# An LSTM layer on one core: one load of 128 rows a step in place of four of 32, and a tail of six Strassen pairs and two plain steps

## The chip, the cores and the metric

The kernel runs on one core of a Trainium2 chip. The metric is the device time of one execution in microseconds (us); of several executions the median is taken. Everything is 32-bit floating point. TensorE (PE) multiplies matrices, VectorE (DVE) and ScalarE (ACT) work on tiles of 128 partitions in the on-chip memory (SBUF) and in the eight accumulation banks of TensorE (PSUM), GpSimd (POOL) does a little elementwise work, and the queue of SyncE (SP) issues nearly all transfers (DMAs) between DRAM and SBUF. A transfer is cut into packets that 16 DMA engines carry.

## The reference

An LSTM over 512 steps with a batch of 32 and 512 inputs and 512 hidden units; the layer's input is added to its output.

```python
xW = jnp.einsum('ntd,dg->ntg', x, Wx) + b          # x is 32 x 512 x 512, Wx is 512 x 2048
def step(carry, xw_t):                             # 512 steps, one after the other
    prev_h, prev_c = carry
    a = xw_t + prev_h @ Wh                         # Wh is 512 x 2048
    i = jax.nn.sigmoid(a[:, :Hd])
    f = jax.nn.sigmoid(a[:, Hd:2 * Hd])
    o = jax.nn.sigmoid(a[:, 2 * Hd:3 * Hd])
    g = jnp.tanh(a[:, 3 * Hd:])
    next_c = f * prev_c + i * g
    next_h = o * jnp.tanh(next_c)
    return ((next_h, next_c), next_h)
return x + hs                                      # hs: all next_h
```

## The kernel before, in words

**The step.** The 512 hidden units are four blocks j of 128. A tile of a step has 128 partitions (j, b): block j, batch row b, 32 rows for each j; its 512 columns are the four gates of the block's units, so that all of a step is one PSUM bank of 128 x 512. `h_part(t)` multiplies the previous h by Wh: 16 instructions of 512 columns, each in one quarter (32 rows) of the array and four of them side by side, into the banks `gbank` (`gbank_72`, `gbank_73`); the trace has two records for each instruction of PE, so that it counts 32. Before that, `seed_step` has ACT copy the step's row of x.Wx + b from SBUF (`xw`) into the bank, so that the product lands on it. `cell` is then the chain of ACT (sigmoid, tanh) and DVE instructions that ends in the transposed h of the next step (`ht`). That chain takes part of the step, and PE fills the wait with work that nothing waits for at once: the products of x and Wx for steps that come later.

**x.Wx.** For the steps 18 to 497 it is made in 15 groups of 32 steps by a scheme of 26 products of sums of blocks, each of which is cut by Strassen's scheme into seven. Its left sums lie in `ubuf`, its right sums are read row by row from DRAM (`vdram`) into a ring of three rows (`vring`), its products go to five PSUM banks (`xbank_66` to `xbank_70`) and to `bbank`, and ACT and DVE add them up (`cbuf`, `r`). Finished blocks of the result are stored to DRAM in `xwd` (`xwd_85` and `xwd_86`, a group each in turn) as [8, 128 rows, 4 blocks j, 512 columns]: the 128 rows are 4 steps by 32 batch rows. `load_xw` reads a step back, at step t that of step t + 3, into one of the three slots of `xw`. This goes on at one pace from about step 20 to step 466; below it is called the stream. The first 18 steps (the head) and the last 14 (the tail, from step 498) have their x.Wx made by other code. From step 469 on (`SPLIT`) a step is done in two halves of 64 hidden units of each block, by 32 instructions of 256 columns, on two pairs of banks (`xbank_66`, `xbank_67` and `gbank_72`, `gbank_73`).

**The tail.** Class `Tail` makes the x.Wx of the last 14 steps between the split steps. Two steps are a pair: Strassen's scheme makes them with seven products instead of eight. A product is eight instructions of 256 columns and is listed as four units, which PE does one by one (eight instructions of 128 columns for two units) or by twos. Plain, a step takes four such products. In the tail `xs_79`, `r_74`, `cbuf`, `ubuf` and a part of `vring` hold the blocks of Wx and their differences, and another part of `vring` the sums of x that the pairs need. The blocks are loaded at the end of the stream: some by `late_loads` at the steps that `LATE` lists, the last six by two calls of `tail.load(3)`, three blocks a call and two DMAs a block. `tail.fill(n)` emits the next n units of the list ahead of the chain of a step, and stops at a unit whose seed or sums don't stand yet.

**The order of the work.** Up to step 20 the instructions are recorded by a planner (`Plan`) that lists each engine's by due times that it estimates. After that each engine's instructions stand in the order in which the program writes them, and each waits for its inputs and for its buffer. SP has one queue for all its DMAs, in program order: a DMA that must wait for its input holds up those behind it.

Of the kernel before, what the change touches and what calls it, by code (L numbers as in the profile page):

```python
# [15 lines left out]
B = 32  # L16
T = 512
NJ = 4
# [4 lines left out]
W = G * P  # L23
HW = G * H
# [15 lines left out]
STREAM0 = HEAD + GS - AHEAD  # L40
END = HEAD + GS * NG - AHEAD
SPLIT = END + 2
LATE = (452, 454, 456, 462, 464, 466, 466)

FIRST = (13, 14, 15)
EARLY = (5, 6, 7, 8, 9, 10, 11, 12, 0, 1, 2, 3, 4, 13, 14, 15)
# [79 lines left out]
class Plan:  # L126
# [57 lines left out]
    def add(self, engine, op, call, out, ins):  # L184
        if not self.live:
            call()
            return
        self.ops.append((engine, op, call, out, ins))
# [220 lines left out]
def kernel(  # L409
# [156 lines left out]
    HALVES = [slice(0, H), slice(H, P)]  # L566

    PAIRS = [[xbank[0], xbank[1]], [gbank[0], gbank[1]]]
    LAST = [xbank[2], xbank[3]]

    def is_split(t):
        return t >= SPLIT
# [481 lines left out]
    def load_xw(t):  # L1054
        dst = xw[:, t % 3]
        if t < HEAD:
            nc.sync.dma_start(out=dst, in_=kept[t - PARKED])
            return
        g, n = divmod(t - HEAD, GS)
        assert group(g).stored[n // 8] == 4, (t, group(g).stored)  # L1060
        m, q = divmod(n, 4)
        for j in range(NJ):
            nc.sync.dma_start(out=dst[j * B : (j + 1) * B], in_=xwd[g % 2][m, q * B : (q + 1) * B, j])

    xw_late = {}

# [112 lines left out]
    class HeadPair:  # L1179
# [28 lines left out]
        def begin(self, first):  # L1208
            step = cbuf[:, 8, 2]
            if first:  # L1210
                sub(step, bias_full[:, HW:W], bias_full[:, 0:HW])
            nc.scalar.copy(self.lo, bias_full[:, 0:HW])
            nc.scalar.copy(self.hi, step)
            a, b = (x_plain(t).rearrange("p (k i) b -> p k i b", i=2) for t in self.steps)
            s1, s2, s3, s4 = (self.sums[:, i] for i in range(4))
            add(s1, b[:, :, 0], b[:, :, 1])
            sub(s2, s1, a[:, :, 0])
            sub(s3, a[:, :, 0], b[:, :, 0])
            sub(s4, a[:, :, 1], s2)
# [56 lines left out]
    class Tail:  # L1276

        def __init__(self):
            self.at = T - TAIL
            self.long_ops = 0.0  # L1280
            self.sums = vring[:, 0, 3:5].rearrange("p n (s k b) -> p n s k b", s=4, k=2)
            self.seed = vring[:, 0, 1:3].rearrange("p k c -> p (k c)")
            self.units = []
            self.results = {}
            self.done = set()
            self.banks = [xbank[2], xbank[3], xbank[4]]
            last = TAIL // 2 - 1
            for kos in ((0,), (1,)):
                for n in (0, 1):
                    self.product(n, 1, kos)  # L1290
            self.after(lambda: self.open(0))
            for n, r in ((2, 1), (0, 2), (1, 2)):
                self.product(n, r)
            self.after(lambda: self.open(1))
            for n in range(last + 1):
                if n > 1:
                    self.product(n, 2)
                if n > 2:
                    self.product(n, 1)
                self.product(n, 5)  # L1300
                self.after(lambda n=n: self.corners(n))
                self.after(lambda n=n: self.top(n))
                if n:
                    self.product(n - 1, 7)
                    self.after(lambda n=n: self.low(n - 1))
                self.product(n, 3)
                if n == 0:
                    self.after(lambda: self.left_sums(1))
                if n < last:
                    self.product(n, 6)  # L1310
                    self.after(lambda n=n: self.right(n))
                if n:
                    self.product(n - 1, 4)
                    self.after(lambda n=n: self.finish(n - 1))
                    if n < last:
                        self.after(lambda n=n: self.begin(n + 1))
            self.product(last, 6)
            self.after(lambda: self.right(last))
            self.paired = len(self.units)
            self.product(last, 7)  # L1320
            self.after(lambda: self.low(last))
            self.product(last, 4)
            self.total = len(self.units)
            self.making = list(range(4))
            self.loading = [b for b in range(2 * NJ) if b in V_OF]

        def steps(self, n):
            return self.at + 2 * n, self.at + 1 + 2 * n

        def after(self, f):  # L1330
            self.units[-1][2].append(f)

        def sum_of(self, blk):
            n = SUMS_AT.index(blk)
# [31 lines left out]
            return self.sum_of(blk)[:, {5: 0, 6: 1, 7: 2, 4: 3}[r]]  # L1366

        def product(self, n, r, kos=(0, 1)):
            needs = {1: "begin" if n > 2 else None, 3: "corners", 6: "corners", 7: "right", 4: "low"}.get(r)
            needs = needs and (needs, n)  # L1370
            for ko in kos:
                for q in range(2):
                    self.units.append((lambda m, ko=ko, q=q: self.matmuls(n, r, ko, q, m), q, [], needs))

        def matmuls(self, n, r, ko, q, m):
            cols = slice(q * P, (q + m) * P)
            bank = self.banks[n % 3]
            dst = bank[:, 0:HW]
            if r == 2:
                dst = bbank[:, n % 2 * HW : (n % 2 + 1) * HW]  # L1380
            elif r in (5, 3):
                dst = bank[:, HW:W]
            for j in range(NJ):
                nc.tensor.matmul(
                    dst[j * B : (j + 1) * B, cols],
                    self.left(n, r, ko),
                    self.right_side(r, ko * 4 + j)[:, cols],
                    start=r == 2 and ko == 0 and q == 0,
                    stop=True,
                    skip_group_check=True,  # L1390
                )

        def start(self, banks):
            for bank in banks:
                nc.scalar.copy(bank[:, 0:HW], bias_full[:, 0:HW])

        def open(self, n):
            if n == 0:
                nc.scalar.copy(self.seed[:, 0:HW], bias_full[:, 0:HW])
                sub(self.seed[:, HW:W], bias_full[:, HW:W], bias_full[:, 0:HW])  # L1400
                self.left_sums(0)
            for bank in self.banks[n : 2 * n + 1]:
                nc.scalar.copy(bank[:, HW:W], self.seed[:, HW:W])

        def begin(self, n):
            self.done.add(("begin", n))
            if n > 2:
                nc.scalar.copy(self.banks[n % 3], self.seed)
            self.left_sums(n)

        def left_sums(self, n):
            self.long_ops = 2000.0 if 0 < n < 3 else 0.0
# [7 lines left out]
        def corners(self, n):  # L1420
            self.done.add(("corners", n))
            self.results[n] = buf_of(take(free_c))
            nc.scalar.copy(self.results[n][:, 0:4:3], self.banks[n % 3].rearrange("p (n c) -> p n c", n=2))

        def top(self, n):
            self.long_ops = 2000.0 if n == 0 else 0.0
# [2 lines left out]

        def right(self, n):  # L1430
            self.done.add(("right", n))
            t, bank = self.results[n], self.banks[n % 3]
            nc.scalar.copy(t[:, 1], bank[:, 0:HW])
            add(t[:, 1], bank[:, HW:W], t[:, 1])
            self.keep(n, 0)

        def low(self, n):
            self.done.add(("low", n))
            t = self.results[n]
            add(t[:, 3], self.banks[n % 3][:, 0:HW], t[:, 3])  # L1440
            if self.steps(n)[1] == T - 1:
                nc.scalar.copy(half_of(T - 1, 1), t[:, 3])

        def finish(self, n):
            t = self.results[n]
            nc.scalar.copy(t[:, 2], self.banks[n % 3][:, 0:HW])
            self.keep(n, 1)

        def keep(self, n, i):
            xw_late[self.steps(n)[i]] = self.results[n][:, 2 * i : 2 * i + 2].rearrange("p s c -> p (s c)")  # L1450

        def share(self, t):
            gone = self.total - len(self.units)
            if gone < self.paired:
                return -(-(self.paired - gone) // max(1, T - 3 - t))
            return -(-(self.total - gone) // max(1, T - 1 - t))

        def fill(self, due):
# [15 lines left out]
    with tc.manual_schedule():  # L1474
# [75 lines left out]
        for t in range(T):  # L1550
# [129 lines left out]
                w_op()  # L1680
            if t == SPLIT - 9:
                late_weights[0] = True
            for _ in range(LATE.count(t)):
                late_loads.pop(0)()
            emit_matmuls(n)
            load_v_ahead()
            if t == SPLIT - 1:
                load_xw(t + 4)
            if END - 1 <= t <= END:
                tail.load(3)  # L1690
            if END <= t < SPLIT:
                tail.start(tail.banks[:2] if t == END else tail.banks[2:])
            done = tail.fill(0 if t < END else max(0, 10 - n // 2) if t < SPLIT else tail.share(t))
            cell(t)
            for f in done:
                f()
# [63 lines left out]
```

## Time and profile before

| | |
|---|---|
| median of 3 executions | 3055.44 us (3054.16 to 3058.35) |
| the profiled execution, its own time | 3056.29 us |
| its span, from the first to the last instruction | 3054.1 us |
| PE busy | 3045.8 us of the span |
| DVE, ACT busy | 2371.6 and 1482.6 us |
| DMA | 754.45 MB in 321,716 packets |
| loads of x.Wx (`xw<-xwd`) | 1920, of 64.0 KB each |
| time from issue to landing of one of them, median | 4.4 us |

How it is to be read. One execution was recorded by the hardware profiler. PE's busy time counts a matmul from its start to its modelled end, and successive ones overlap, so that PE reads as busy nearly everywhere; an idle stretch of PE shows in its own timeline with the engine that it waited for in brackets. All instructions are issued through one helper, so that every one has the line number L146, and groups are told apart by their tiles: `xw<-xwd` is a DMA that writes the tile `xw` and reads `xwd`. The digits of the line DMA are the mean busy share of the 16 DMA engines in tenths, in 40 equal slices of the span; they do not show one engine apart from another.

### The profile page before, as it was taken

The numbers are of one execution on the slowest core, as the hardware profiler recorded it, in microseconds if no ns is written. First come the engines' busy times: TensorE is split into PE (matmuls) and PEld (weight loads), VectorE is DVE, ScalarE is ACT, GpSimd is POOL, SyncE is SP. The second block draws the span as 40 slices with busy tenths as digits, with TensorE's granted clock in tenths as the row PEclk, the third lists the DMA queues.
The fourth block names the chain that finished last, engine by engine and source line by source line (L and its number), as shares of the span: only waits on it lengthen the run. The fifth ranks groups of instructions, "written<-read, shape, count | busy, mean of one in ns | idle before, by whom it ended". The sixth has DMA issues, their size and how long they took to land.

```text
span 3054.1 us, 107775 instructions
## 1 busy us (share of the span) xinstructions
PE 3045.8 (100%) x43344; PEld 1624.6 (53%) x43344; DVE 2371.6 (78%) x6556; ACT 1482.6 (49%) x5527; POOL 222.4 (7%) x473
## 2 busy tenths in 40 slices
PE   9999999999999999999999999999999999999999
PEld 6445555555555555555555555555555555555666
DVE  8778787887878878787787877878778787787765
ACT  2445444454454544545445454454544445454454
POOL 0000000000000000000000000000000000000000
PEclk9999999999999999999999999999999999999999
DMA  9988887787877878778787777777777777778630
GB/s 356 312 282 284 257 271 242 249 260 239 266 242 244 272 229 272 238 246 266 236 269 239 247 261 243 257 249 251 257 242 259 242 255 255 247 255 276 199 97 18
DMA packets 321716, 754.45 MB, mean 247 GB/s; under 512 B 51136, under 2 KB 106432, under 8 KB 320704
## 3 DMA queue, kind: packets, MB, share of 16 engines
q1 hardware_dynamic: 321072, 747.54, 74.8%
q8 instruction: 342, 5.60, 0.8%
q14 instruction: 158, 1.29, 0.2%
q10 hardware_dynamic: 144, 0.01, 0.0%
HBM read 565.94 MB, written 184.55 MB: 246 GB/s over the span
## 4 chain that ended last, share of the span: by engine, by line
PE 97%; DMA 1%; DVE 1%; SPq 0%; ACT 0%; issue 0%; ACTq 0%; DVEq 0%
PE gbank L146 54%; PE xbank L146 37%; PE bbank L146 6%; DMA xwd<-cbuf 0%; DMA ubuf<-vdram 0%; SPq L146 0%; DMA vring<-vdram 0%; DMA xnat<-in_x_dram 0%; DVE cbuf L146 0%; DVE prod L146 0%; DVE ubuf L146 0%; DMA xw<-xwd 0%; DVE s L146 0%; ACT s L146 0%; DVE hbuf L146 0%
## 5 line engine op out<-in xcount | busy, mean ns | idle before, releaser
L146 PE MATMUL gbank<-wh_sb,ht 128*32 128x512 f32 x14912 | 1697.6, 592 | 0.5
L146 PEld LDWEIGHTS gbank<-wh_sb,ht 128*32 128x32 f32 x14912 | 552.6, 110 | 807.3 <-issue 699.9
L146 ACT ACTIVATE s<-gbank 128x128 f32<-128x128 f32 (+1 forms) x1920 | 331.6, 257 | 1191.4 <-PE gbank L146 1189.9
L146 PE MATMUL xbank<-vring,ubuf 128*32 128x256 f32 (+1 forms) x13584 | 849.1, 368 | 0.0
L146 PEld LDWEIGHTS xbank<-vring,ubuf 128*32 128x32 f32 x13584 | 521.1, 110 | 297.2 <-issue 134.9
L146 DVE TENSOR_TENSOR prod<-s 128x128 f32<-128x128 f32 (+2 forms) x1093 | 296.9, 278 | 461.5 <-ACT s L146 457.1
L146 POOL TENSOR_TENSOR oc<-xnat,ht 128x128 f32<-128x128 f32 x469 | 222.2, 474 | 2637.4 <-DVE ht L146 1328.5
L146 ACT ACTIVATE tanh_c<-s 128x64 f32<-128x64 f32 (+1 forms) x921 | 236.9, 258 | 187.5 <-DVE s L146 184.3
L146 ACT COPY cbuf<-xbank 128x256 f32<-128x256 f32 (+1 forms) x692 | 287.8, 439 | 33.2 <-PE xbank L146 26.2
L146 ACT COPY gbank<-xw 128x512 f32<-128x512 f32 (+1 forms) x487 | 285.6, 589 | 1.6 <-DMA xw<-xwd 1.1
L146 DVE STREAM_TRANSPOSE ht<-hbuf 128x64 f32<-128x64 f32 (+1 forms) x921 | 226.8, 246 | 64.4 <-DVE hbuf L146 1.8
L146 DVE TENSOR_TENSOR s<-prod 128x64 f32<-128x64 f32 (+1 forms) x1007 | 227.4, 226 | 34.2
L146 DVE TENSOR_TENSOR cbuf<-xbank,cbuf 128x256 f32<-128x256 f32 x461 | 181.3, 409 | 41.6 <-ACT cbuf L146 39.5
L146 DVE TENSOR_TENSOR cbuf<-cbuf 128x1024 f32<-128x1024 f32 x171 | 208.8, 1224 | 0.7
L146 PE MATMUL xbank<-vring,r 128*32 128x256 f32 (+1 forms) x3216 | 208.3, 357 | 0.0
L146 PE MATMUL xbank<-vring,xs 128*32 128x256 f32 (+1 forms) x3120 | 201.9, 356 | 0.0
L146 DVE TENSOR_TENSOR hbuf<-o,tanh_c 128x64 f32<-128x64 f32 (+1 forms) x921 | 190.5, 207 | 4.6 <-ACT tanh_c L146 4.0
L146 ACT COPY r<-xbank 128x256 f32<-128x256 f32 (+1 forms) x425 | 180.8, 438 | 16.0 <-PE xbank L146 14.1
L146 PE MATMUL bbank<-vring,ubuf 128*32 128x256 f32 (+1 forms) x2600 | 184.4, 342 | 0.0
L146 PEld LDWEIGHTS xbank<-vring,r 128*32 128x32 f32 x3216 | 122.6, 110 | 79.6 <-issue 46.2
L146 ACT ACTIVATE o<-gbank 128x128 f32<-128x128 f32 (+1 forms) x508 | 154.7, 305 | 12.7 <-PE gbank L146 12.7
L146 PEld LDWEIGHTS xbank<-vring,xs 128*32 128x32 f32 x3120 | 118.9, 110 | 59.7 <-issue 22.9
(194 smaller groups left out, 2290.1 us busy)
## 6 DMA issues: line engine op xcount, KB each, us to landing
vring<-vdram SPq DMA_DIRECT2D x310, 896.0 KB, 5.8
xw<-xwd SPq DMA_DIRECT2D x1920, 64.0 KB, 4.4
xwd<-cbuf SPq DMA_DIRECT2D x139, 512.0 KB, 4.4
xwd<-r SPq DMA_DIRECT2D x86, 512.0 KB, 4.4
out_dram<-oc SPq DMA_DIRECT2D x255, 128.0 KB, 3.8
xnat<-in_x_dram SPq DMA_DIRECT2D x63, 512.0 KB, 5.3
xs<-in_x_grouped_dram SPq DMA_DIRECT2D x45, 512.0 KB, 4.8
vring<-vdram SPq DMA_DIRECT2D x33, 512.0 KB, 4.8
```

What stands on the lines that cost most here:

```text
L146: self.plan.add(self.name, op, lambda: call(*args, **kw), out, rest)
```

## The change

Two things are changed.

`load_xw` loads a step with one DMA. Before, a loop over j issued four, each of 32 rows of 2 KB: batch rows 0 to 31 of block j, to 32 neighbouring partitions. Now the block of DRAM is read as [j, b, columns], and one DMA of 256 KB writes all 128 partitions. In DRAM a row of the step (j, b) still lies 2 KB from the next j and 8 KB from the next b. As the instruction carries them, the pattern of the source has 4 blocks (2 KB apart) of 32 rows (8 KB apart) of 512 columns, and that of the destination 128 partitions of 512 columns. Before, both patterns had 32 rows of 512 columns.

The tail's 14 steps become a plain step (498), six pairs (499 to 510) and another plain step (511), where they were seven pairs: 4 + 42 + 4 = 50 products where there were 49. The plain products of step 498 and a quarter of those of 511 go to the bank `xbank_68`; the pairs have two banks in turn (`xbank_69` and `xbank_70`) where they had three. The plain products need no sums of x. The results of two pairs' steps are told of at once (`finish`), step 511 is seeded with what is finished of it and the rest of its products are added to its own banks (`plain_last`, `seed_last`). `tail.load(3)` is called at steps 467 and 468 instead of 466 and 467, one load of weights in `LATE` moves from step 466 to 467, and the number of units ahead of the chains of 467 and 468 may be up to 13 instead of 10 (`SPLIT` and `END` stay at 469 and 467).

```diff
@@ constants @@
-LATE = (452, 454, 456, 462, 464, 466, 466)
+LATE = (452, 454, 456, 462, 464, 466, 467)
...
-    LAST = [xbank[2], xbank[3]]
+    LAST = [xbank[3], xbank[4]]
@@ load_xw @@
         m, q = divmod(n, 4)
-        for j in range(NJ):
-            nc.sync.dma_start(out=dst[j * B : (j + 1) * B], in_=xwd[g % 2][m, q * B : (q + 1) * B, j])
+        nc.sync.dma_start(out=dst, in_=xwd[g % 2][m, q * B : (q + 1) * B].rearrange("b j c -> j b c"))
@@ class Tail @@
             self.units = []
+            self.late = []
             self.results = {}
             self.done = set()
-            self.banks = [xbank[2], xbank[3], xbank[4]]
+            self.banks = [xbank[3], xbank[4]]
             last = TAIL // 2 - 1
-            for kos in ((0,), (1,)):
-                for n in (0, 1):
-                    self.product(n, 1, kos)
-            self.after(lambda: self.open(0))
-            for n, r in ((2, 1), (0, 2), (1, 2)):
-                self.product(n, r)
-            self.after(lambda: self.open(1))
-            for n in range(last + 1):
+            self.plain(self.at, (0,))
+            self.after(lambda: self.begin(0))
+            self.plain(self.at, (1, 2, 3))
+            self.product(0, 1)
+            self.product(0, 2)
+            self.after(lambda: self.begin(1))
+            self.product(1, 2)
+            self.product(1, 1)
+            for n in range(last):
                 if n > 1:
                     self.product(n, 2)
-                if n > 2:
                     self.product(n, 1)
                 self.product(n, 5)
                 self.after(lambda n=n: self.corners(n))
                 self.after(lambda n=n: self.top(n))
-                if n:
+                if n == 0:
+                    self.plain(T - 1, (0,))
+                else:
                     self.product(n - 1, 7)
                     self.after(lambda n=n: self.low(n - 1))
                 self.product(n, 3)
                 if n == 0:
                     self.after(lambda: self.left_sums(1))
-                if n < last:
-                    self.product(n, 6)
-                    self.after(lambda n=n: self.right(n))
+                self.product(n, 6)
+                self.after(lambda n=n: self.right(n))
                 if n:
                     self.product(n - 1, 4)
                     self.after(lambda n=n: self.finish(n - 1))
-                    if n < last:
+                    if n + 1 < last:
                         self.after(lambda n=n: self.begin(n + 1))
-            self.product(last, 6)
-            self.after(lambda: self.right(last))
+            self.product(last - 1, 7)
+            self.after(lambda: self.low(last - 1))
+            self.product(last - 1, 4)
+            self.after(lambda: self.finish(last - 1))
+            self.after(self.seed_last)
             self.paired = len(self.units)
-            self.product(last, 7)
-            self.after(lambda: self.low(last))
-            self.product(last, 4)
+            self.plain_last((1, 2, 3))
             self.total = len(self.units)
             self.making = list(range(4))
             self.loading = [b for b in range(2 * NJ) if b in V_OF]
 
         def steps(self, n):
-            return self.at + 2 * n, self.at + 1 + 2 * n
+            return self.at + 1 + 2 * n, self.at + 2 + 2 * n
 
         def after(self, f):
             self.units[-1][2].append(f)
+
+        def plain(self, t, chunks):
+            bank = xbank[2]
+            needs = ("plain", self.at) if t > self.at else None
+            for c in chunks:
+                for q in range(4):
+                    self.units.append((lambda m, c=c, q=q: plain_part(t, c, q, m, bank, True), q % 2, [], needs))
+            if chunks[-1] == 3 or t == T - 1:
+                self.after(lambda: self.whole(t, bank))
+
+        def plain_last(self, chunks):
+            for c in chunks:
+                for q in range(4):
+                    half = q // 2
+                    emit = lambda m, c=c, q=q, half=half: plain_part(T - 1, c, q, m, LAST[half], place=q % 2)
+                    self.units.append((emit, q % 2, [], ("seeded", T - 1)))
+
+        def seed_last(self):
+            self.done.add(("seeded", T - 1))
+            for i in range(2):
+                nc.scalar.copy(half_of(T - 1, i), xw_late[T - 1][:, i * HW : (i + 1) * HW])
+
+        def whole(self, t, bank):
+            self.done.add(("plain", t))
+            nc.scalar.copy(self.room(t), bank)
+            if t == self.at:
+                nc.scalar.copy(bank, bias_full)
+
+        def room(self, t):
+            if not self.late:
+                buf = buf_of(take(free_c))
+                self.late += [buf[:, 0:2], buf[:, 2:4]]
+            xw_late[t] = self.late.pop(0).rearrange("p s c -> p (s c)")
+            return xw_late[t]
 
         def sum_of(self, blk):
             n = SUMS_AT.index(blk)
...
-        def start(self, banks):
-            for bank in banks:
-                nc.scalar.copy(bank[:, 0:HW], bias_full[:, 0:HW])
-
-        def open(self, n):
+        def begin(self, n):
+            self.done.add(("begin", n))
             if n == 0:
                 nc.scalar.copy(self.seed[:, 0:HW], bias_full[:, 0:HW])
                 sub(self.seed[:, HW:W], bias_full[:, HW:W], bias_full[:, 0:HW])
-                self.left_sums(0)
-            for bank in self.banks[n : 2 * n + 1]:
-                nc.scalar.copy(bank[:, HW:W], self.seed[:, HW:W])
...
+            nc.scalar.copy(self.banks[n % 2], self.seed)
+            if n != 1:
+                self.left_sums(n)
...
-                return -(-(self.paired - gone) // max(1, T - 3 - t))
+                return -(-(self.paired - gone) // max(1, T - 4 - t))
@@ the loop over the steps @@
-            for _ in range(LATE.count(t)):
+            if t in LATE:
                 late_loads.pop(0)()
             emit_matmuls(n)
             load_v_ahead()
             if t == SPLIT - 1:
                 load_xw(t + 4)
-            if END - 1 <= t <= END:
+            if END <= t < SPLIT:
+                assert pos[0] == 4 * len(items)
                 tail.load(3)
-            if END <= t < SPLIT:
-                tail.start(tail.banks[:2] if t == END else tail.banks[2:])
-            done = tail.fill(0 if t < END else max(0, 10 - n // 2) if t < SPLIT else tail.share(t))
+            if t == END:
+                nc.scalar.copy(xbank[2], bias_full)
+            done = tail.fill(0 if t < END else max(0, 13 - n // 2) if t < SPLIT else tail.share(t))
```

How it moves instructions, at three places. The first is the queue of SP in the middle of the stream, around the switch of a load from `xwd_85` to `xwd_86`. Before:

```order
L146 DMA out_dram<-oc_98 128x256
L146 DMA xw<-xwd_85 32x512 x4
L146 DMA xwd_86<-cbuf 128x2x512
L146 DMA vring<-vdram 128x512
L146 DMA vring<-vdram 128x1280
L146 DMA xw<-xwd_86 32x512 x4
L146 DMA out_dram<-oc_99 128x256
```

and now:

```order
L146 DMA out_dram<-oc_98 128x256
L146 DMA xw<-xwd_85 128x1x512
L146 DMA xwd_86<-cbuf 128x2x512
L146 DMA vring<-vdram 128x512
L146 DMA vring<-vdram 128x1280
L146 DMA xw<-xwd_86 128x1x512
L146 DMA out_dram<-oc_99 128x256
```

Nothing changes place there; each group of four loads is one.

The second is the same queue at the stream's end, where the tail's last blocks of Wx (`ubuf`, `vring`) are loaded in two lots of three. Before:

```order
L146 DMA ubuf<-vdram 128x3x256
L146 DMA ubuf<-vdram 128x256
L146 DMA ubuf<-vdram 128x3x256
L146 DMA ubuf<-vdram 128x256
L146 DMA xw<-xwd_85 32x512 x4
L146 DMA ubuf<-vdram 128x3x256
L146 DMA ubuf<-vdram 128x256
L146 DMA ubuf<-vdram 128x3x256
L146 DMA ubuf<-vdram 128x256
L146 DMA vring<-vdram 128x3x256
L146 DMA vring<-vdram 128x256
L146 DMA out_dram<-oc_99 128x256
```

and now:

```order
L146 DMA ubuf<-vdram 128x3x256
L146 DMA ubuf<-vdram 128x256
L146 DMA out_dram<-oc_99 128x256
L146 DMA xw<-xwd_85 128x1x512
L146 DMA xwd_85<-r_74 128x2x512
L146 DMA xw<-xwd_85 128x1x512
L146 DMA ubuf<-vdram 128x3x256
L146 DMA ubuf<-vdram 128x256
L146 DMA ubuf<-vdram 128x3x256
L146 DMA ubuf<-vdram 128x256
L146 DMA vring<-vdram 128x3x256
L146 DMA vring<-vdram 128x256
```

The second lot, which ends in `vring`, now stands a step later: behind a store of the output, a store of a block (`xwd_85<-r_74`) and two loads of steps, where it had one load ahead of it.

The third is PE from the first split step (469, the instructions `xbank_66<-wh_sb,ht_96` just ahead of these rows) on. Before:

```order
L146 MATMUL bbank<-xs_79,seeds_own 32x256 x2
L146 MATMUL bbank<-r_74,seeds_own 32x256
L146 MATMUL bbank<-cbuf,seeds_own 32x256
L146 MATMUL xbank_68<-ubuf,vring 32x256 x4
L146 MATMUL xbank_68<-ubuf,vring 32x128 x3
L146 MATMUL xbank_68<-vring 32x128
L146 MATMUL gbank_72<-wh_sb,vring 32x256 x8
```

and now:

```order
L146 MATMUL bbank<-xs_79,seeds_own 32x256 x6
L146 MATMUL bbank<-r_74,seeds_own 32x256
L146 MATMUL bbank<-cbuf,seeds_own 32x256
L146 MATMUL xbank_70<-xs_79,seeds_own 32x128 x4
L146 MATMUL gbank_72<-wh_sb,vring 32x256 x8
L146 MATMUL gbank_73<-wh_sb,vring 32x256 x4
L146 MATMUL gbank_72<-wh_sb,vring 32x256 x8
L146 MATMUL gbank_73<-wh_sb,vring 32x256 x12
L146 MATMUL xbank_70<-xs_79,seeds_own 32x128 x4
L146 MATMUL xbank_70<-xs_79,seeds_own 32x256 x2
L146 MATMUL xbank_70<-r_74,seeds_own 32x256
L146 MATMUL xbank_70<-cbuf,seeds_own 32x256
```

The first product that reads the late blocks (`ubuf`, and behind it `vring`) stood between the steps 469 and 470. Now only products of blocks that came earlier (`xs_79`, `r_74`, `cbuf`) stand there, and the first that reads `ubuf` follows behind these rows, between 470 and 471.

More of the change, by code (lines that the diff above doesn't have):

```diff
@@ L1368, in product @@
         def product(self, n, r, kos=(0, 1)):
-            needs = {1: "begin" if n > 2 else None, 3: "corners", 6: "corners", 7: "right", 4: "low"}.get(r)
+            needs = {1: "begin", 3: "corners", 6: "corners", 7: "right", 4: "low"}.get(r)
             needs = needs and (needs, n)
@@ L1376, in matmuls @@
             cols = slice(q * P, (q + m) * P)
-            bank = self.banks[n % 3]
+            bank = self.banks[n % 2]
             dst = bank[:, 0:HW]
@@ L1400, in open @@
                 sub(self.seed[:, HW:W], bias_full[:, HW:W], bias_full[:, 0:HW])
-                self.left_sums(0)
-            for bank in self.banks[n : 2 * n + 1]:
-                nc.scalar.copy(bank[:, HW:W], self.seed[:, HW:W])
[L1405 to L1409, printed above, removed]
+            nc.scalar.copy(self.banks[n % 2], self.seed)
+            if n != 1:
+                self.left_sums(n)
         def left_sums(self, n):
@@ L1422, in corners @@
             self.results[n] = buf_of(take(free_c))
-            nc.scalar.copy(self.results[n][:, 0:4:3], self.banks[n % 3].rearrange("p (n c) -> p n c", n=2))
+            nc.scalar.copy(self.results[n][:, 0:4:3], self.banks[n % 2].rearrange("p (n c) -> p n c", n=2))
         def top(self, n):
@@ L1431, in right @@
             self.done.add(("right", n))
-            t, bank = self.results[n], self.banks[n % 3]
+            t, bank = self.results[n], self.banks[n % 2]
             nc.scalar.copy(t[:, 1], bank[:, 0:HW])
             add(t[:, 1], bank[:, HW:W], t[:, 1])
-            self.keep(n, 0)
         def low(self, n):
@@ L1439, in low @@
             t = self.results[n]
-            add(t[:, 3], self.banks[n % 3][:, 0:HW], t[:, 3])
-            if self.steps(n)[1] == T - 1:
-                nc.scalar.copy(half_of(T - 1, 1), t[:, 3])
+            add(t[:, 3], self.banks[n % 2][:, 0:HW], t[:, 3])
         def finish(self, n):
             t = self.results[n]
[L1446 to L1450, printed above, removed]
+            nc.scalar.copy(t[:, 2], self.banks[n % 2][:, 0:HW])
+            for i, step in enumerate(self.steps(n)):
+                xw_late[step] = t[:, 2 * i : 2 * i + 2].rearrange("p s c -> p (s c)")
         def share(self, t):
```

## The prediction

> **What bounds the kernel now.** I read the page first: busy time, chain of waits, transfers.
>
> ```profile
> span 3054.1 us, 107775 instructions
> PE 3045.8 (100%) x43344; PEld 1624.6 (53%) x43344; DVE 2371.6 (78%) x6556; ACT 1482.6 (49%) x5527; POOL 222.4 (7%) x473
> PE 97%; DMA 1%; DVE 1%; SPq 0%; ACT 0%; issue 0%; ACTq 0%; DVEq 0%
> DMA packets 321716, 754.45 MB, mean 247 GB/s; under 512 B 51136, under 2 KB 106432, under 8 KB 320704
> xw<-xwd SPq DMA_DIRECT2D x1920, 64.0 KB, 4.4
> ```
>
> PE is busy for 3045.8 of 3054.1 us, and 97% of the chain that ended last is PE. So a gain can come only from the 8.3 us in which PE is idle, or from fewer PE instructions. A loss can come from anything that falls behind PE. What has least room? The table by stage (us, then busy us of PE, PEld, DVE, ACT, POOL, the granted clock, the DMA share, GB/s) says it:
>
> ```profile
> 0.00:75.00 75.00, 73.85 (x1180) 46.21 (x1184) 66.86 (x127) 18.60 (x54) 6.42 (x9) 1.00 0.97 355
> 1000.00:2000.00 1000.00, 999.89 (x13852) 523.55 (x13848) 786.75 (x2136) 494.33 (x1836) 77.98 (x170) 1.00 0.77 252
> 2850.00:2900.00 50.00, 47.72 (x860) 32.59 (x856) 36.25 (x142) 24.56 (x110) 1.25 (x2) 1.00 0.62 196
> 2900.00:3054.00 154.00, 149.65 (x2792) 101.92 (x2784) 90.53 (x452) 79.68 (x364) 0.00 (x0) 1.00 0.19 58
> ```
>
> In the middle PE idles 0.11 us in 1000, while the 16 DMA engines are busy for 77% of the time: DVE (79%) and they are the nearest to a bound. PE's idle time lies at the ends: 1.15 us in the first row, 2.28 in the third, 4.35 in the last. For the stream alone (180 to 2850 us) the view of the transfers gives:
>
> ```profile
> DMA packets 275386, 676.19 MB, mean 253 GB/s; under 512 B 45694, under 2 KB 83580, under 8 KB 274953
> q1 hardware_dynamic: 274953, 670.25, 77.1%
> q8 instruction: 292, 4.78, 0.7%
> q14 instruction: 141, 1.16, 0.2%
> xw<-xwd SPq DMA_DIRECT2D x1803, 64.0 KB, 4.5
> ```
>
> **Part 1, the load: what it frees.** SP's queue in the stream, and ACT's copies of the loaded rows:
>
> ```profile
> 1004.76 2.28 SPq L146 DMA_DIRECT2D xw<-xwd  x4
> 1007.13 0.38 SPq L146 DMA_DIRECT2D vring<-vdram  x1
> 1007.61 3.12 SPq L146 DMA_DIRECT2D xw<-xwd  x4
> ```
> ```profile
> 1015.03 0.61 ACT L146 COPY gbank<-xw 128x512 f32<-128x512 f32 x1
> 1020.84 0.59 ACT L146 COPY gbank<-xw 128x512 f32<-128x512 f32 x1
> ```
>
> Four issues hold SP for 2.28 to 3.12 us a step; one should take about the 0.38 us of the load beside it. So some 2 to 2.7 us of SP in each 5.81 us step are freed, 451 times (1803 / 4). It is worth nothing in the stream: PE loses no time there for SP to give back. The cover is the three slots of `xw`: a load is issued about two steps (11.6 us) before its copy and lands in 4.5.
>
> **Part 1, the load: what it costs.** The bytes stay the same. What may change is over how many of the 16 engines a load is spread. The trace hints at the present spreading. In the window of 2900 to 2950 us (head line of its transfers, then its issues), 44 + 6 + 1 + 1 = 52 DMAs have 807 packets under 512 B, 15.5 a DMA, though most are loads of 32 rows:
>
> ```profile
> DMA packets 3318, 4.74 MB, mean 95 GB/s; under 512 B 807, under 2 KB 1575, under 8 KB 3308
> xw<-xwd SPq DMA_DIRECT2D x44, 64.0 KB, 2.0
> out_dram<-oc SPq DMA_DIRECT2D x6, 128.0 KB, 2.1
> xwd<-cbuf SPq DMA_DIRECT2D x1, 512.0 KB, 2.7
> xnat<-in_x_dram SPq DMA_DIRECT2D x1, 512.0 KB, 3.9
> ```
>
> I read that as one closing packet for each of 16 engines: a load of 32 rows gives every engine two. The DMAs of before have an outermost count of 32, 128 or 512 on both sides, so 16 always divides it. The new load's source starts with 4 blocks, its destination with 128 partitions. If engines are dealt out by the outermost count, only four can share it, 64 KB each; if by rows, 16 as now. The trace has no DMA of the first kind. The nearest row of the second is `kept`, whose source is 128 plain rows:
>
> ```profile
> xw<-kept SPq DMA_DIRECT2D x5, 256.0 KB, 4.9
> ```
>
> I take four engines, the same four each time, as the likelier: the counts of the pattern are what the issue carries, and the flat rows of `kept` are not what it is given here.
>
> The Trainium skill, "DMA: Bandwidth & Descriptors", section "Why a DMA increments its semaphore by 16 and not by 1", states this as the rule: the largest number up to 16 that divides the slowest dimension of both patterns as carried, and on this kind of queue the lowest-numbered engines. By it the load gets engines 0 to 3; the 15.5 packets agree for 32 rows, and no run here shows a 4. The same page's "Rules for kernel authors" also advises to coalesce small transfers, which taken alone would speak for the change.
>
> What four engines would carry. Evenly spread, each engine now moves 676.19 / 16 = 42.26 MB in the 2670 us. Of these, 1803 x 65,536 bytes / 16 = 7.39 MB are the loads; on four engines these get 4 x 7.39, so 42.26 + 3 x 7.39 = 64.42 MB each. The price of a MB has three rows:
> - In the stream a MB takes an engine 0.78 x 2670 / 42.26 = 49.3 us (0.78: the three queues' 77.1, 0.7 and 0.2%). Four engines then need 3175 us, 505 more than the 2670.
> - In the first 75 us, with the engines full at 0.97, it takes 0.97 x 16 / 355 GB/s = 43.7 us: 2816 us, 146 more.
> - The fastest slice in the stream (of 0.75 us each, from 1000 to 1030 us) moves 411 GB/s, 16 / 411 = 38.9 us per MB: 2508 us, 162 less than the 2670, so just covered.
>
> ```profile
> GB/s 178 302 391 406 371 309 128 332 328 310 262 163 311 307 371 327 262 374 240 355 307 403 347 275 68 371 337 145 359 318 363 272 287 347 161 161 299 411 374 337
> ```
>
> The full row (43.7) is nearest to four engines with a queue that never empties. But the stream also makes SP wait for results ahead of stores, and the row has no such gaps. I take a quarter of the way from 43.7 to 49.3: 2816 + 90 = 2906 us, **+236 us**. This is by far the largest term. What is late then: `vring`, whose rows PE's filler reads, and with it the `h_part` queued behind the filler; and ACT's copy of `xw`, behind which the sigmoids of the step stand on ACT, then the chain on DVE and again `h_part`.
>
> **Part 2, the tail.** It has 50 products for 49. A step there is 64 records of `h_part` and 16 of one product:
>
> ```profile
> 2989.74 3.66 PE L146 MATMUL gbank<-wh_sb,vring 128*32 128x256 f32 x64
> 2993.19 0.85 PE L146 MATMUL xbank<-ubuf,vring 128*32 128x256 f32 x11
> 2994.07 3.66 PE L146 MATMUL xbank<-wh_sb,vring 128*32 128x256 f32 x64
> ```
>
> From 2989.74 to 2994.07 are 4.33 us for 80 records, 0.054 each; 16 more cost **+0.87 us**. PE's stalls at the switch:
>
> ```profile
> 2863.80 0.41 PE L146 MATMUL xbank<-ubuf,vring 128*32 128x128 f32 x2 [0.22 <-DMA ubuf<-vdram]
> 2865.84 0.30 PE L146 MATMUL xbank<-vring 128*32 128x128 f32 x1 [1.63 <-DMA vring<-vdram]
> 2870.34 3.66 PE L146 MATMUL xbank<-wh_sb,vring 128*32 128x256 f32 x64 [0.43 <-DVE prod L146]
> ```
>
> They make up the 2.28 us of the third stage. Products of blocks that are there already now stand in their place, and the first reader of `ubuf` comes a step later: **-2.28 us**. The loads come later too, behind a block's store and two loads of steps. The second lot took from 2856.81 to its `vring` reader at 2865.84, some 9 us:
>
> ```profile
> 2856.81 2.62 SPq L146 DMA_DIRECT2D ubuf<-vdram  x4
> 2859.47 0.96 SPq L146 DMA_DIRECT2D vring<-vdram  x2
> ```
>
> If issued some 1.5 us later, as the store's wait would have it, it lands near 2867.3, just before the reader one step on (2863.8 + 4.4 = 2868.2). I put a new stall between 0 and 1 us, **+0.5**. The edits of seeds and sums move short ACT and DVE work under PE's 4.33 us a step: nothing, and some tenths if one chain were late. Part 2 gives -0.9 us.
>
> **Sum.** The profiled execution took 3056.29 us, 2.2 more than its span and 0.85 above the median shown. 3056.29 + 236 - 0.9 = 3291.4, and 3290.5 on the median's scale, say **3290 us**.
>
> **The rivals.**
> - *Sixteen engines, or four that take turns.* The load is dealt out by rows, or each DMA starts at another engine: every engine keeps 42.26 MB, at 78%. Then only part 2 is left, and the median is 3055.4 - 0.9 = 3054.5, not slower. It decides as soon as a load's bytes are spread evenly over some steps: a single load on four engines (64 KB each, 2.8 us at 43.7 us per MB) still lands within 11.6 us. For it: the row of `kept`. Against: the counts that the issue carries.
> - *Four engines, just covered.* At 38.9 us per MB they are busy for 94%: PE waits only where transfers bunch. With nothing lost it is 3054.5; with a wait like the longest at the switch (1.63 us) in each of the 15 groups of 32 steps, 3079. Against: that price is one slice's, and the full row has 43.7.
> - *Four engines, at the stream's present price:* 3055.4 + 505 - 0.9 = 3559.5. For it: 49.3 is what these very packets take now. Against: part of that time is the start of a transfer on an idle engine, which a full queue hides.
> - *Faster.* It takes 6 of the 8.3 us of PE's idle time, and the 4.35 us at the end are the last step's chain and store, which stay.
>
> **How the numbers follow.** A measurement of this kernel can tell 0.2% (6.1 us) from no change. Four engines that bound the stream: 0.68, with 3120 to 3560 as their own range. Four engines just covered: 0.08, of which 0.05 is slower by over 0.2% and 0.03 within. Sixteen, or taking turns: 0.21, within. Faster: 0.03. So faster 0.03, same 0.24, slower 0.73. The range has to reach the even spreading below, 3050, and leaves out the dearest end above: 3050 to 3500.
>
> **What would show it.** Four engines: PE's busy share falls evenly over 180 to 2850 us, with waits of PE on `vring<-vdram` and of ACT on `xw<-xwd`; the loads land well above 4.5 us; GB/s and the mean DMA share fall together; the packets under 512 B fall from 64 a step to 4, by 480 x 60 = 28,800 of 51,136. Sixteen engines: they fall by 480 x 48 = 23,040, with a landing near 4.9 us and PE full. Part 2: no wait for `ubuf` or `vring` at the switch above 1 us, and steps of 4.33 us behind it. I am wrong if the small packets fall by 28,800 and PE stays full, or if the stream is slower with loads on 16 engines.

## The result, and the profile after

The changed kernel takes 3177.99 us (median of five, 3168.95 to 3181.74) where the kernel before takes 3056.19 (3054.16 to 3058.35): 1.0393 times as long, 95% interval 1.0382 to 1.0405. It is slower by some 122 us. The forecast was slower, 3290 us, with a range of 3050 to 3500: the direction and the mechanism hold, the size of the loss was put at nearly twice what it is. The range reached down to no change, so a time inside it says little by itself; the signs below say more.

The page of the changed kernel: span, busy time, the DMA engines in 40 slices, packets, chain of waits, the group of ACT's copies of the loads, and the loads' issues.

```profile
span 3179.9 us, 105745 instructions
PE 3082.5 (97%) x43344; PEld 1614.6 (51%) x43344; DVE 2370.1 (75%) x6549; ACT 1510.2 (47%) x5526; POOL 222.9 (7%) x473
DMA  9978777776776777777777777777777777677530
DMA packets 292901, 754.21 MB, mean 237 GB/s; under 512 B 22336, under 2 KB 77632, under 8 KB 291904
PE 17%; DMA 5%; DVE 1%; ACT 0%; SPq 0%; issue 0%; DVEq 0%; ACTq 0%
L146 ACT COPY gbank<-xw 128x512 f32<-128x512 f32 (+1 forms) x487 | 280.8, 579 | 675.6 <-DMA xw<-xwd 674.7
xw<-xwd SPq DMA_DIRECT2D x480, 256.0 KB
```

PE has the same number of records, and the bytes are nearly the same; PE is idle for 97.4 us instead of 8.3, and its busy time is 36.7 us longer. The packets under 512 B fell from 51,136 to 22,336, by exactly 28,800: from 64 closing packets a step to 4. ACT's copies into `gbank`, which before waited 1.1 us in all for the loads, wait 674.7. Before, 97% of the chain was PE; now only about a quarter of the span could be followed, with 17% in PE and 5% in DMA. The mean of the 16 engines hides the cause: it is lower than before.

By stage (us, busy us of PE, PEld, DVE, ACT, POOL, granted clock, DMA share, GB/s), of the changed kernel:

```profile
75.00:180.00 105.00, 105.00 (x1604) 51.81 (x1600) 85.84 (x163) 49.17 (x130) 6.46 (x10) 1.00 0.92 312
180.00:300.00 120.00, 111.96 (x1568) 55.12 (x1556) 87.69 (x227) 52.38 (x189) 9.44 (x17) 0.97 0.76 250
400.00:1000.00 600.00, 584.04 (x8021) 301.54 (x8016) 455.21 (x1238) 291.21 (x1061) 45.37 (x99) 1.00 0.74 243
2200.00:2850.00 650.00, 628.54 (x8568) 322.36 (x8572) 490.64 (x1329) 311.91 (x1136) 48.28 (x106) 0.99 0.73 242
```

and of the kernel before, one stage:

```profile
400.00:1000.00 600.00, 600.00 (x8296) 313.55 (x8292) 473.87 (x1283) 293.75 (x1094) 46.81 (x102) 1.00 0.77 250
```

PE is full until the stream begins, then loses 8 us in the first 120 (6.7%), and 2.7 and 3.3% in the two later stages shown. In the 600 us from 400 on PE did 8021 records; the kernel before does 8296 there. The DMA share and the GB/s fell together there, from 0.77 to 0.74 and from 250 to 243. The waits, and a few steps on ACT, on PE and in SP's queue (the wait before each in brackets):

```profile
ACT gbank L146 <- DMA xw<-xwd: 674.7, 362, 5.8
PE gbank L146 <- DVE hbuf L146: 44.4, 49, 2.2
PE xbank L146 <- DMA vring<-vdram: 20.2, 14, 6.7
```
```profile
1016.41 1.11 ACT L146 COPY r<-xbank 128x256 f32<-128x256 f32 x3
1021.79 0.59 ACT L146 COPY gbank<-xw 128x512 f32<-128x512 f32 x1 [4.26 <-DMA xw<-xwd]
1022.31 0.66 ACT L146 ACTIVATE s<-gbank 128x128 f32<-128x128 f32 x4
1022.84 0.30 ACT L146 ACTIVATE o<-gbank 128x128 f32<-128x128 f32 x1
```
```profile
1017.04 3.64 PE L146 MATMUL gbank<-wh_sb,ht 128*32 128x512 f32 x32
1020.47 0.64 PE L146 MATMUL bbank<-vring,xs 128*32 128x256 f32 x8
1020.90 2.16 PE L146 MATMUL xbank<-vring,ubuf 128*32 128x256 f32 x40
1024.38 3.64 PE L146 MATMUL gbank<-wh_sb,ht 128*32 128x512 f32 x32 [1.32 <-DVE hbuf L146]
```
```profile
1006.47 4.53 SPq L146 DMA_DIRECT2D xw<-xwd  x2
```

PE had done with `h_part` and begun its filler at 1020.47, but the sigmoids of the step start at 1022.31: they stand on ACT behind the copy of the next step's row, and that copy waited 4.26 us for its load. So the load of the next step holds up the chain of this one, then `ht`, and PE, which stands idle for 1.32 us before its next `h_part`. The views give no landing times for these loads. But `xw` has three slots, and by their order the row copied at 1021.79 is the one whose load was issued at 1006.47: it took some 15 us to land, where the median in the stream was 4.5.

### The profile page after: what moved, and what is told of

It reads as the page before. It is cut to its first block, busy times and chain, and to the rows that moved or that the text cites. A ratio compares the mean times of both kernels' runs of the same rounds, so it can differ in the third digit from the quotient of the medians.

```text
span 3179.9 us, 105745 instructions
## 1 busy us (share of the span) xinstructions
PE 3082.5 (97%) x43344; PEld 1614.6 (51%) x43344; DVE 2370.1 (75%) x6549; ACT 1510.2 (47%) x5526; POOL 222.9 (7%) x473
## 2 busy tenths in 40 slices
DMA packets 292901, 754.21 MB, mean 237 GB/s; under 512 B 22336, under 2 KB 77632, under 8 KB 291904
## 5 line engine op out<-in xcount | busy, mean ns | idle before, releaser
L146 PE MATMUL gbank<-wh_sb,ht 128*32 128x512 f32 x14912 | 1706.5, 595 | 45.9 <-DVE hbuf L146 44.4
L146 PE MATMUL xbank<-vring,ubuf 128*32 128x256 f32 (+1 forms) x13584 | 858.7, 370 | 36.9 <-DMA vring<-vdram 19.7
L146 ACT COPY gbank<-xw 128x512 f32<-128x512 f32 (+1 forms) x487 | 280.8, 579 | 675.6 <-DMA xw<-xwd 674.7
```

The costliest lines, as they stand in the source:

```text
L146: self.plan.add(self.name, op, lambda: call(*args, **kw), out, rest)
```

## The experiments

Three questions: which part of the change costs the time, whether it is the number of DMA engines or something else of the one large DMA, and whether the loss is a matter of capacity. The figures below are medians; each ratio is to the kernel before on the same chip.

### The two parts apart

`e1_load_only` is the kernel before with the new load:

```diff
-        for j in range(NJ):
-            nc.sync.dma_start(out=dst[j * B : (j + 1) * B], in_=xwd[g % 2][m, q * B : (q + 1) * B, j])
+        nc.sync.dma_start(out=dst, in_=xwd[g % 2][m, q * B : (q + 1) * B].rearrange("b j c -> j b c"))
```

> The kernel before with the new load alone, the tail with its seven pairs. Theory A (the load goes over four of the 16 DMA engines, and these four bound the stream): the whole loss comes from the load, 3170 to 3190 us, with 22,336 packets under 512 B and ACT's copies waiting some 670 us for the loads, as after the change. Rival B (the tail or the two together cost most of it): within 10 us of 3056.

3171.7 us, 1.0376 (1.0362 to 1.0390), 22,336 packets under 512 B, ACT's copies waiting 628.9 us. The load is the loss; that the time comes out 6 us below that of the whole change is not clear of noise, since the two intervals of the ratio overlap.

`e2_tail_only` is the changed kernel with that edit taken back, so the new tail alone.

> The changed kernel with the four loads of 32 rows put back: the new tail alone. Theory A with the sum of the prediction for the tail (+0.87 for a product, -2.28 of stalls, +0 to 1 for a new one): 3053.5 to 3056.5 us, and PE's waits for ubuf and vring at the switch gone. Rival B (the tail costs part of the loss): above 3065.

3054.25 us against 3056.04, 0.9992 (0.9983 to 1.0001): not to be told from no change by its time, but by its profile. Its stage of the switch, three DMA issues there, and PE's readers of the late blocks:

```profile
2850.00:2900.00 50.00, 50.00 (x920) 34.92 (x916) 36.95 (x140) 26.00 (x112) 1.24 (x2) 1.00 0.66 203
```
```profile
2861.55 2.69 SPq L146 DMA_DIRECT2D xw<-xwd  x4
2864.34 1.92 SPq L146 DMA_DIRECT2D ubuf<-vdram  x4
2866.30 0.96 SPq L146 DMA_DIRECT2D vring<-vdram  x2
```
```profile
2869.56 0.64 PE L146 MATMUL xbank<-ubuf,vring 128*32 128x256 f32 x8
2873.49 0.38 PE L146 MATMUL xbank<-vring 128*32 128x256 f32 x1
```

PE is busy for all 50 us where it was for 47.72: the stalls of 2.28 us are gone and none took their place. Three steps further on, from 2975.03 to 2988.00, take 4.32 to 4.33 us each, as forecast. The second lot of blocks is issued 7.5 us later than before (2864.34 for 2856.81), not 1.5, but the reader of `vring` moved as far, from 2865.84 to 2873.49.

### The number of engines

`e3_flat_after` keeps one DMA of 256 KB and 128 rows, and lays the rows out so that they are evenly spaced. The 128 columns of a product's left side are put batch row first (an order of the input), and `xwd` is [8, block j, 128 rows, columns]; the stores follow that layout, and the planner's record of what a DMA touches is made to cover every row of `xwd`. The two lines of the change that bear on the load:

```diff
-        nc.sync.dma_start(out=dst, in_=xwd[g % 2][m, q * B : (q + 1) * B].rearrange("b j c -> j b c"))
+        nc.sync.dma_start(out=dst, in_=xwd[g % 2][m].rearrange("j (b q) c -> q (j b) c", q=4)[q])
...
-    xwd = [dram.tile([2 * MB, P, NJ, W], F32, name=f"xwd_{i}") for i in range(2)]
+    xwd = [dram.tile([2 * MB, NJ, P, W], F32, name=f"xwd_{i}") for i in range(2)]
```

The source of a load is then 128 rows of 512 columns, 8 KB apart, where it was 4 blocks of 32 rows 8 KB apart.

> The changed kernel, still with one load of 128 rows and 256 KB a step, 8 KB from row to row in DRAM as now, but with the rows of a step laid out in DRAM so that the source too is one run of 128 evenly spaced rows (the 128 rows of a group are ordered batch row first, block j outermost). Theory A (spreading goes by the outermost count of both sides, here 128 and 128): 16 engines, 3053.5 to 3057 us, 28,096 packets under 512 B, landing near 5 us. Rival C (one DMA of 256 KB a step is late for itself, whatever its engines: one completion for all rows, one place in the queue): near 3178, packets under 512 B also 28,096 or fewer.

3054.61 us, 0.9995 (0.9986 to 1.0004). Its page:

```profile
DMA packets 298661, 754.23 MB, mean 247 GB/s; under 512 B 28096, under 2 KB 83392, under 8 KB 297664
xw<-xwd SPq DMA_DIRECT2D x480, 256.0 KB, 4.9
```

28,096 packets under 512 B are 16 a load. All of the loss is gone with one DMA a step. So neither the size of the DMA nor its one completion made the loads late.

`e4_flat_before` is the same load in the kernel before, with its tail of seven pairs.

> The kernel before (tail of seven pairs) with the flat load of 128 rows over 16 engines. Theory A: 3054 to 3057 us, no measurable difference from before, since PE lost no time to SP's queue; the stalls at the switch of 0.2 to 1.6 us may shrink with SP freed. If the freed SP queue is worth something in the stream: below 3050. Rival C: near 3178.

3054.93 us, 0.9995 (0.9986 to 1.0004): the SP time that one DMA in place of four frees is worth nothing that can be measured.

`e3` also changed the order of the rows in DRAM. `e8_padded` keeps that order and takes away the even spacing alone, by four unused rows behind each block j (against e3):

```diff
-    xwd = [dram.tile([2 * MB, NJ, P, W], F32, name=f"xwd_{i}") for i in range(2)]
+    xwd = [dram.tile([2 * MB, NJ, P + 4, W], F32, name=f"xwd_{i}") for i in range(2)]
...
-        nc.sync.dma_start(out=dst, in_=xwd[g % 2][m].rearrange("j (b q) c -> q (j b) c", q=4)[q])
+        nc.sync.dma_start(out=dst, in_=xwd[g % 2][m, :, 0:P].rearrange("j (b q) c -> q j b c", q=4)[q])
```

> The kernel of e3 with four unused rows behind each block j in DRAM: the same 128 rows of 2 KB a load, still 8 KB from row to row, one DMA of 256 KB; but the 128 rows are no longer evenly spaced, so that the source has 4 blocks of 32 rows again. Theory A (the outermost count of the pattern sets the number of engines): back to 3165 to 3185 us with 22,336 packets under 512 B. Rival D (e3 gained by the order of the rows in DRAM, of loads or of stores): it stays within 10 us of e3's 3054.6.

3224.17 us, 1.0551 (1.0535 to 1.0567), and 22,336 packets under 512 B:

```profile
DMA packets 292901, 754.21 MB, mean 234 GB/s; under 512 B 22336, under 2 KB 77632, under 8 KB 291904
ACT gbank L146 <- DMA xw<-xwd: 790.8, 369, 5.5
```

The same rows, in the same order and 8 KB apart within a block: with 4 x 32 in the pattern the loss is back. It is 46 us larger than the changed kernel's, which no theory had expected; the last experiment takes that up.

`e7_two_of_64` loads each step from 24 on by two DMAs of 64 rows, whose source has 2 blocks of 32 rows (the steps before by four DMAs):

```diff
-        nc.sync.dma_start(out=dst, in_=xwd[g % 2][m, q * B : (q + 1) * B].rearrange("b j c -> j b c"))
+            for j in (0, 2):
+                nc.sync.dma_start(
+                    out=dst[j * B : (j + 2) * B],
+                    in_=xwd[g % 2][m, q * B : (q + 1) * B, j : j + 2].rearrange("b j c -> j b c"),
+                )
...
```

> Two DMAs of 64 rows a step (source: 2 blocks of 32 rows). Theory A (spreading goes by the outermost count, here 2, and always to the same engines): two engines carry 42.26 + 7 x 7.39 = 94 MB each; at 43.7 us per MB the stream takes 4108 us for 2670: some 4490 us in all, with 64 rows or closing packets counted 2 a DMA, 20,500 packets under 512 B. Rival M (two DMAs take turns over engines): no slower than the 3178 of the changed kernel. Rival N (it is the number of rows or bytes per DMA that makes a load late): between 3056 and 3178.

4351.11 us, 1.4233 times as long (1.4205 to 1.4262). Its page, and a stage:

```profile
PE 3439.8 (79%) x43344; PEld 1634.3 (38%) x43344; DVE 2369.7 (55%) x6549; ACT 1481.6 (34%) x5526; POOL 221.6 (5%) x473
DMA packets 293265, 754.24 MB, mean 173 GB/s; under 512 B 22696, under 2 KB 77992, under 8 KB 292264
1000.00:2000.00 1000.00, 781.90 (x9352) 356.24 (x9348) 534.52 (x1447) 333.51 (x1240) 52.56 (x115) 0.90 0.53 170
```

Smaller DMAs and more of them, and a loss ten times as large: 22,696 small packets are two for each of 948 loads of 64 rows, 64 for each of the six steps by fours, and the 20,416 that are left of the 51,136 of before without its 480 x 64. (The 20,500 expected is hardly more than these 20,416: it left the loads' own packets out.) If the two engines changed from DMA to DMA, every engine would carry no more than before. So it is the same two. And a DMA still puts 64 KB on each of its engines, as in the changed kernel, so the loss is not one of each DMA by itself either.

### Capacity, or a price for each load

`e5_half` takes the one DMA over four engines for every second step from 24 on, and four of 32 rows for the others; `e6_three_quarters` for three steps of four.

```diff
-        nc.sync.dma_start(out=dst, in_=xwd[g % 2][m, q * B : (q + 1) * B].rearrange("b j c -> j b c"))
+        if t >= 24 and t % 2:
+            nc.sync.dma_start(out=dst, in_=xwd[g % 2][m, q * B : (q + 1) * B].rearrange("b j c -> j b c"))
+            return
+        for j in range(NJ):
+            nc.sync.dma_start(out=dst[j * B : (j + 1) * B], in_=xwd[g % 2][m, q * B : (q + 1) * B, j])
```

> The changed kernel in which, from step 24 on, every second step is loaded by the one DMA over four engines and the others by four of 32 rows. Theory A (four engines are full): each of the four carries 42.26 + 22.16 / 2 = 53.3 MB; at the 43.7 us per MB of the full row that is 2331 us of the stream's 2670, so they keep up: 3054 to 3062 us. Rival L (a load on four engines is late for itself and costs the same each time): half of the 122 us, 3115.

3064.49 us, 1.0026 (1.0017 to 1.0036).

> Three of four steps by the one DMA over four engines. Theory A: 42.26 + 0.75 x 22.16 = 58.9 MB, 2573 us of 2670, 96%: near full, so 3055 to 3090 us, since transfers bunch. Rival L: three quarters of the 122 us, 3146.

3070.36 us, 1.0053 (1.0036 to 1.0070). Three quarters of the loads cost 16 us above the 3054.25 of the tail alone, the last quarter 108 more. That is a bound being passed, not a price for each load. But half the loads cost 10 us, 2.5 more than the end of the range for capacity. The stages of e5 show where:

```profile
180.00:300.00 120.00, 118.80 (x1668) 58.91 (x1664) 93.82 (x242) 57.16 (x203) 10.48 (x19) 1.00 0.83 261
300.00:400.00 100.00, 94.78 (x1292) 46.05 (x1288) 69.84 (x197) 45.91 (x171) 7.33 (x16) 0.98 0.83 248
400.00:1000.00 600.00, 599.89 (x8294) 303.35 (x8288) 471.57 (x1280) 294.38 (x1098) 46.33 (x101) 1.00 0.79 252
```

and the same of the kernel before:

```profile
180.00:300.00 120.00, 120.00 (x1692) 59.87 (x1685) 94.51 (x245) 57.37 (x207) 10.50 (x19) 1.00 0.86 277
300.00:400.00 100.00, 100.00 (x1388) 52.25 (x1380) 75.70 (x210) 48.75 (x183) 7.81 (x17) 1.00 0.83 263
```

The loss lies between 180 and 400 us, where the kernel moves more than later (277 and 263 GB/s, and some 250 behind it). `e9_half_late` starts the alternation at step 60, behind that stretch.

> The kernel of e5 with the one DMA over four engines for every second step from step 60 on instead of from 24. In e5 PE was short of 6.4 us between 180 and 400 us (118.80 of 120 and 94.78 of 100), where the kernel before moves 277 and 263 GB/s, and of 0.1 us between 400 and 1000. Theory A (four engines are over their capacity only where the other transfers are dense): 3054 to 3058 us, with PE full from 180 to 400 us. Rival L (a loss for each load): 3063 or more.

3058.27 us, 1.0008 (0.9999 to 1.0016), just above the range, and PE is full from 180 to 400 us (120.00 and 100.00). So some 6 of the 10 us were that stretch. The four that stay are in no single place: in the profiles 1.8 us of PE's idle time are in 2000 to 2850 us (0.6 in the tail alone) and 0.3 at the switch, and PE's busy time is 1.4 us longer than that of the tail alone (3047.5 and 3046.1). What causes them is not settled.

### The 46 us of the padded layout

`e10_padded5` is e8 with `P + 5` for `P + 4`, one more unused row. In e8 the blocks j lie 264 KB apart, 33 times the 8 KB from row to row; now 266 KB.

> The kernel of e8 with five unused rows behind each block j instead of four. With four, the rows that the four engines read at the same time lie 264 KB apart, a multiple of the 8 KB from row to row; with five they lie 266 KB apart, so that they differ by 2 KB, 4 KB and 6 KB within 8 KB, as in the changed kernel. Theory R (e8's 46 us above the changed kernel come from rows that meet in the same place of DRAM): 3165 to 3190 us. Rival S (they come from something else of the layout, such as the stores): 3215 to 3235.

3175.20 us, 1.0381 (1.0364 to 1.0399): the time of the changed kernel. ACT's copies wait 667.9 us for the loads, where they waited 790.8 in e8. So one row of 2 KB is worth 49 us, and the range of rival S is missed. Loads and stores carry the same bytes in the same patterns in both; but the row moves the places that the stores write as well as those that the loads read (the two halves of a store lie 1056 KB apart in e8 and 1064 KB in e10), so which of the two it works through is not shown.

## Why the prediction was right, and where its size was off

**The bound.** It named the 16 DMA engines as that which has least room beside PE, and the stage table as the place to see it. That held.

**Four engines, the same four.** Held, by three signs: 28,800 small packets fewer; the loss gone with 128 evenly spaced rows (e3) and back with four blocks (e8) at the same size, order and distance; and two engines with two blocks (e7). No view shows one engine apart from another, so the numbers 16, 4 and 2 are read from the small packets, and that the four are always the same from the loss. The Trainium skill's rule in "DMA: Bandwidth & Descriptors" ("Why a DMA increments its semaphore by 16 and not by 1"), the largest number up to 16 that divides the outermost dimension of both patterns, agrees with 16, 4 and 2 engines here. The evidence from `kept` for sixteen was no evidence: its source is flat, and flat rows do get 16 (e3).

**The price of a MB: the term that was mis-sized.** The step "I take a quarter of the way from 43.7 to 49.3" is the error. With the whole loss put down to the stream, it took 2670 + 123.7 = 2794 us (3177.99 less the 3054.25 of the tail alone), which over 64.42 MB is 43.4 us per MB; the forecast's 2906 had 45.1. With two engines it is (2670 + 1296.9) / (42.26 + 7 x 7.39) = 42.2. So full engines cost what the full row of the first 75 us says, and a little less, in spite of SP's waits in the stream: the share of engines that are seldom full (49.3) is no measure of what they can carry. The full row alone would have given 3056.29 + 146 - 0.9 - 0.85 = 3200 us. At 43.4 the four engines fill the 2670 us at 61.5 MB: between the 58.9 of e6, which loses 16 us, and the 64.4 of the change, which loses 124.

**What is late.** Both candidates are in the trace. Of PE's own waits 44.4 us end with the chain (`hbuf`) that starts behind the copy of `xw`, and 20.2 with `vring`. The 674.7 us that ACT's copies wait are not to be set against these, since PE has its filler meanwhile.

**The tail.** -0.9 us were expected, -1.8 measured, inside what can't be told from no change. The stalls of 2.28 us went as argued; the new stall of 0.5 did not come, since the reader of `vring` moved with its load (the estimate had the load 1.5 us later and the reader 2.4). The estimate and the run both have one product more, 0.87 us by the estimate.

**The rivals.** "Sixteen engines" is what e3 is, and its 3054.5 is met by 3054.61. "Just covered" asked for 38.9 us per MB, which one slice of 0.75 us shows and no run sustains. "The stream's present price" fell with the term above. SP's freed time was put at nothing, and e4 has nothing; the one issue takes 0.53 us, where 0.38 was put.

## What to carry to other kernels

Before fewer and larger DMAs replace many, read the outermost count of both patterns of the new one: here it went with the number of engines (128 or 32: sixteen, 4: four, 2: two; only the source's count fell below 16), and the mean share of the engines did not show that some were full. A cheap sign is in the page: in all these runs the packets under 512 B came to the number of engines for each load. And price a bound by a row in which the resource is full; its busy time per MB where it idles a fifth of the time overstated the price here (49.3 for 43.4).

## What was not expected of the hardware

**Rows that may meet.** With four engines reading four blocks side by side, blocks 264 KB apart cost 49 us more than blocks 266 KB apart (3224.17 and 3175.20), rows being 8 KB apart in both; in the changed kernel the blocks lie 2 KB apart. So this one distance, 33 times that of the rows, cost some 1.7% of the stream; no other multiple of 8 KB was tried with four engines. The Trainium skill's page "DMA: Bandwidth & Descriptors" ("Latency and other measured facts") tells of slow row distances of large powers of two and of a padding that cures them, and infers that rows then meet in a channel of the DRAM. Here it would be the distance between what the engines read at one time, and the slow one is no power of two; that they meet in one channel is a guess here too.

**PE's own work gets longer in the runs in which it waits.** In e7 the same 43,344 records keep PE busy for 3439.8 us instead of 3045.8, and the granted clock is 0.90 in the stage shown, where it is 1.00 before. So of the 1294 us by which its span is longer, 394 are not idle time of PE. Two `h_part` of e7, and the stages that they fill:

```profile
1026.42 3.64 PE L146 MATMUL gbank<-wh_sb,ht 128*32 128x512 f32 x32
1034.87 5.34 PE L146 MATMUL gbank<-wh_sb,ht 128*32 128x512 f32 x32 [0.23 <-DVE hbuf L146]
```
```profile
1026.42:1030.06 3.64, 3.64 (x40) 1.42 (x36) 2.28 (x5) 1.08 (x2) 0.44 (x1) 1.00 0.64 200
1034.87:1040.21 5.34, 5.34 (x40) 1.93 (x44) 3.68 (x7) 0.19 (x1) 0.45 (x1) 0.68 0.62 186
```

The same 32 records take longer just as the granted clock falls: 3.64 / 0.68 = 5.35. All records of `h_part` together took 275 us more than before (1972.9 and 1697.6). Over the span of e7 the mean clock is 0.921, so the clock can account for at most 0.079 x 4347.8 = 343 of the 394 us. In the changed kernel PE's busy time is 36.7 us longer, of 126 us of span, and with a mean clock of 0.994 at most some 19 of them are the clock. What the rest is, and what makes the clock fall, was not tested.
